# The first sequence's rows are turned in the last group of the experts, and TensorE works the experts' stage in written order

## The chip, the cores and the metric

The kernel runs on one core of one Trainium2 chip. Its time is the device time of that core in microseconds (us) from start to end of one execution; the time before is the median of three runs. Beside them one further execution was profiled, and every line and duration shown comes from that one. TensorE is called PE in the profile, VectorE DVE, ScalarE ACT, GpSimd POOL and SyncE SP; PEld is PE's loading of weights.

## The reference, cut to what matters

Four steps are added to x in turn, 32 sequences of 256 tokens with 128 features: causal attention of 16 heads, a mixture of 16 experts and a shared one, attention by hyperbolic distance, and a feed-forward. The two in the middle are what the change touches (all in fp32):

```python
# experts: 16 of width 64, the best 4 (of the best 2 of 4 groups) weighted, and a shared expert
g = einsum('th,eih->eti', xn, gate_proj);  u = einsum('th,eih->eti', xn, up_proj)
y = einsum('tkh,tk->th', einsum('eti,ehi->eth', silu(g) * u, down_proj)[topk_idx], topk_weight)
x = x + y + (silu(xn @ sg.T) * (xn @ su.T)) @ sd.T

# hyperbolic attention, 16 heads of 8; c = 1
q, k, v = (heads(layernorm(x) @ w.T) for w in (wq, wk, wv))
diff_sq = |q|^2 + |k|^2 - 2 q.k
denom   = maximum((1 - |q|^2) * (1 - |k|^2), 1e-6)
dist    = arccosh(maximum(1 + 2 * diff_sq / denom, 1))
x = x + (softmax(-dist) @ v) @ wo.T
```

Since exp(-arccosh(z)) is z - sqrt(z^2 - 1), a weight of the softmax is such a difference, and its sum comes with the product with the values by a column of ones. Where all |q|^2 and |k|^2 are large enough, the bounds of `denom` and of `z` never act, and 1 / (1 - |q|^2) can be worked into the rows of the queries and keys beforehand. That is the "far path".

## The kernel before, in words

The 8192 tokens are 16 groups (g) of 512; a group is 4 tiles of 128 tokens, or two sequences. x lies in SBUF from the start to the end. The stages follow each other: causal attention (PE in an order written by hand), then experts with the survey, then a branch, then the far path (or another path, which this data does not take).

**Experts (L658).** The first and second layers of two experts at a time make one chunk (c) of 128 rows: 8 chunks and the shared expert, 9 per group. Per chunk there are the products g (L696) and u (L698) into PSUM, Silu on ACT (L700), the multiplication with u (L701) and with the routing weights wb (L703) on DVE, and the product that sums into y (L704). The routing weights come by DMA: each is spread over 64 partitions, 2 MB per group, fetched by SP at chunk 1 of the group before into one of three buffers. When a group's nine sums are done, ACT copies y (L708), PE transposes it and DVE adds it to x (`add_transposed`, L109 and L110). Between them lie the pieces of the routing of the last four groups (`preparation`), one after every odd chunk while there are any.

**Survey (L605).** Of each group, once its x is done: statistics on DVE (L612, L613), x less its mean on POOL (sxn, L614), four transposes on PE (xc, L620), a copy on ACT (L622) and a store of the centred, turned rows to DRAM (L623), the product with the query and key weights in two halves (sqk, L628), its squares on ACT (L633), their sums by head on DVE (L634); then the group's smallest and largest norm (L638, L639) and ra = 1 / (1 - norm) (L641, L642). `survey_result` (L644) makes one flag of all groups' extremes, and the branch at L1451 reads it.

The order of this stage on each engine is not the written one: a planner takes the instructions and sets the order per engine by its own costs. It can put a group's first products between the last steps of the group before.

**Far path (L987).** It is in written order on PE, ACT, DVE and POOL. The rows of queries and keys of one sequence are made in one tile each, qa and ka: a head has 32 places, of which 8 hold the scaled query or key (`scaled`, L1070, with the factors co = ra / deviation), two hold the "last rows" (`last_rows`, L1075 to L1078: a - 1 and a for the query, -0.5 b and 0.5 - 0.5 b for the key; four operations on POOL), and the rest stays zero. `turned` (L1103) transposes them four heads at a time, so that the score product (L1123) has tokens along the free dimension. For one step, a quarter of a sequence's heads, there follow: scores on PE, -4 x scores clipped at zero on ACT (ft, L1177), a product on DVE (fv, L1183), a root on ACT (L1188), the difference on POOL in four operations (L1193), and the product with the values on PE (fav, L1135). The scores of the next step wait for this step's DVE product, since each has its PSUM buffer for itself. The start is outside the loop, in `run` (L1292): the centred rows of group 0 are loaded, sequence 0 is multiplied, scaled and turned, sequence 1 multiplied and scaled, and then the first scores are made.

Of the kernel before, what the change touches and what calls it, by code (L numbers as in the profile page):

```python
# [9 lines left out]
F32 = mybir.dt.float32  # L10
# [6 lines left out]
P = 128  # L17
# [23 lines left out]
class Net:  # L41
# [551 lines left out]
    def survey_tiles(self, keep, dram):  # L593

        self.w_qkv, self.w_o = self.load(keep, "w_qkv", self.nc.sync), self.load(keep, "w_o", self.nc.sync)

        self.xc = [dram.tile([P, GT], F32, name=f"xc{g}") for g in range(NG)]

        self.rv = keep.tile([P, NG, TG], F32, name="rv")
        self.ra = keep.tile([P, NG, TG, 2, H], F32, name="ra")  # L600

        self.ends = keep.tile([P, 2, NG], F32, name="ends")
        self.flag = keep.tile([1, 1], mybir.dt.int32, name="flag")

    def survey(self, pool, psum, g):  # L605

        nc = self.nc
        mv = pool.tile([P, TG, 2], F32, tag="smv", name=f"smv{g}")
        xn = pool.tile([P, TG, D], F32, tag="sxn", bufs=1, name=f"sxn{g}")
        for t in range(TG):  # L610
            st = pool.tile([P, nc.vector.BN_STATS_DIM], F32, tag="sst", bufs=4, name=f"sst{g}_{t}")
            nc.vector.bn_stats(st, self.xg[g][:, t, :])  # L612
            nc.vector.bn_aggr(mv[:, t, :], st)  # L613
            nc.gpsimd.tensor_scalar(xn[:, t, :], self.xg[g][:, t, :], mv[:, t, 0:1], None, ALU.subtract)  # L614
        rv = self.rv[:, g]
        nc.vector.tensor_scalar(rv, mv[:, :, 1], EPS, None, ALU.add)
        nc.vector.reciprocal(rv, rv)
        ps = psum.tile([P, GT], F32, tag="w", name=f"xc_ps{g}")
        for t in range(TG):
            nc.tensor.transpose(ps[:, t * P : (t + 1) * P], xn[:, t, :], self.ident)  # L620
        xc = pool.tile([P, GT], F32, tag="sxc", name=f"sxc{g}")
        nc.scalar.copy(xc, ps)  # L622
        nc.sync.dma_start(out=self.xc[g], in_=xc)  # L623
        n2 = pool.tile([P, TG, 2 * H], F32, tag="sn2", name=f"sn2_{g}")
        for i in range(2):
            qk = psum.tile([P, 2, 2 * D], F32, tag="w", name=f"sqk{g}_{i}")
            for t in range(2):
                nc.tensor.matmul(  # L628
                    qk[:, t], xc[:, (2 * i + t) * P : (2 * i + t + 1) * P], self.w_qkv[:, 0 : 2 * D],
                    start=True, stop=True,  # L630
                )
# [3 lines left out]
                n2[:, 2 * i : 2 * i + 2], sq.rearrange("p t (h d) -> p t h d", d=DH), AX.X, ALU.add  # L635
            )
        nc.vector.tensor_mul(n2, n2, rv.unsqueeze(2).to_broadcast([P, TG, 2 * H]))
        nc.vector.tensor_reduce(self.ends[:, 0, g : g + 1], n2, AX.XY, ALU.min)  # L638
        nc.vector.tensor_reduce(self.ends[:, 1, g : g + 1], n2, AX.XY, ALU.max)  # L639
        ra = self.ra[:, g].rearrange("p t s h -> p t (s h)")  # L640
        nc.vector.tensor_scalar(ra, n2, -1.0, 1.0, ALU.mult, ALU.add)  # L641
        nc.vector.reciprocal(ra, ra)  # L642
# [15 lines left out]
    def experts(self, prep):  # L658
# [3 lines left out]
        with (  # L662
# [18 lines left out]

            pieces = self.preparation(NG // QUAD - 1, prep, psum, "w")
            ready = fetched(0)
            for g in range(NG):
                xT, wb = ready
                y_ps = psum.tile([P, GT], F32, tag="y", name=f"y_ps{g}")
                for c in range(NCH + 1):
                    if c == 1 and g + 1 < NG:
                        ready = fetched(g + 1)
                    shared = c == NCH  # L690
                    m = INTER if shared else P
                    wg = s_g if shared else w_g[:, c * P : (c + 1) * P]
                    wu = s_u if shared else w_u[:, c * P : (c + 1) * P]
                    wd = s_d if shared else w_d[:, c, :]
                    g_ps = psum.tile([P, GT], F32, tag="g", name=f"g_ps{g}_{c}")
                    nc.tensor.matmul(g_ps[:m, :], wg, xT, start=True, stop=True)  # L696
                    u_ps = psum.tile([P, GT], F32, tag="u", name=f"u_ps{g}_{c}")
                    nc.tensor.matmul(u_ps[:m, :], wu, xT, start=True, stop=True)  # L698
                    act = pool.tile([P, GT], F32, tag="act", bufs=3, name=f"act{g}_{c}")
                    nc.scalar.activation(act[:m, :], g_ps[:m, :], AF.Silu)  # L700
                    nc.vector.tensor_mul(act[:m, :], u_ps[:m, :], act[:m, :])  # L701
                    if not shared:
                        nc.vector.tensor_mul(act, act, wb[:, c])  # L703
                    nc.tensor.matmul(y_ps, wd, act[:m, :], start=c == 0, stop=shared)  # L704
                    if c % 2 == 1 and pieces:
                        pieces.pop(0)()
                yT = pool.tile([P, GT], F32, tag="yT", name=f"yT{g}")
                nc.scalar.copy(yT, y_ps)  # L708
                self.add_transposed(pool, psum, "u", g, yT)
                self.survey(pool, psum, g)  # L710
# [276 lines left out]
    def far_attention(self):  # L987
# [20 lines left out]
        with (  # L1008
# [3 lines left out]
        ):  # L1012
            vas = []
# [5 lines left out]

            qa = wp.tile([P, 2, H, ROWS], F32, name="fqa")  # L1020
            ka = wp.tile([P, 2, H, ROWS], F32, name="fka")
            nc.vector.memset(qa, 0.0)
            nc.vector.memset(ka, 0.0)
# [14 lines left out]
            xcs = {}  # L1038

            def centred(g):  # L1040
                xcs[g] = pool.tile([P, GT], F32, tag="xc", name=f"fxc{g}")
                nc.sync.dma_start(out=xcs[g], in_=self.xc[g])
# [13 lines left out]
            def queries_keys(b):  # L1056
                g, ts = chunks(b)
                qk = bank([P, 2, 2, D], f"fqk{b}")
                for t in range(2):
                    i = ts.start + t  # L1060
                    nc.tensor.matmul(
                        qk[:, t], xcs[g][:, i * P : (i + 1) * P], w_qkv[:, 0 : 2 * D], start=True, stop=True
                    )
                return qk.rearrange("p t s (h d) -> p t s h d", h=H)

            def scaled(b, heads, co):
                g, ts = chunks(b)
                for s, x in enumerate((qa, ka)):
                    f = co[:, ts, s].unsqueeze(3).to_broadcast([P, 2, H, DH])
                    nc.vector.tensor_mul(x[:, :, :, 0:DH], heads[:, :, s], f)  # L1070

            def last_rows(b):
                g, ts = chunks(b)
                a, k = (self.ra[:, g, ts, s].unsqueeze(3) for s in range(2))
                nc.gpsimd.tensor_scalar(qa[:, :, :, 8:9], a, 1.0, None, ALU.subtract)  # L1075
                nc.gpsimd.tensor_copy(qa[:, :, :, 9:10], a)
                nc.gpsimd.tensor_scalar(ka[:, :, :, 8:9], k, -0.5, None, ALU.mult)
                nc.gpsimd.tensor_scalar(ka[:, :, :, 9:10], k, -0.5, 0.5, ALU.mult, ALU.add)  # L1078
# [19 lines left out]
            def turned(b, x, hg):  # L1098

                ps = bank([P, 2, N], f"fT_ps{b}_{hg}")  # L1100
                for j in range(2):
                    for t in range(2):
                        nc.tensor.transpose(  # L1103
                            ps[:, j, t * P : (t + 1) * P],
                            x[:, t, (hg + j) * HG : (hg + j + 1) * HG, :].rearrange("p h r -> p (h r)"),
                            self.ident,
                        )
                return ps
# [180 lines left out]
            oTs, sas, sTs, cos = {}, {}, {}, {0: factors(0)}  # L1289
            centred(0)  # L1290

            def run():  # L1292
                scaled(0, queries_keys(0), cos[0])
                last_rows(0)
                rows_of = row_tiles(0)
                for x, to in ((ka, rows_of[1]), (qa, rows_of[0])):
                    for hg in range(0, NHG, 2):
                        (nc.scalar.copy if hg else nc.vector.tensor_copy)(to[hg // 2], turned(0, x, hg))
                last_rows(1)
                scaled(1, queries_keys(1), cos[0])  # L1300
                sc = scores(0, 0, rows_of)

                fours = {}
                for n in range(NHG * (B + 2)):
# [18 lines left out]
                    if s in (1, 2):  # L1323
                        if ahead is not None:
                            nc.vector.tensor_copy(next_rows[s % 2][0], turned(ahead, (qa, ka)[s % 2], 0))
# [7 lines left out]
                    if s in (1, 2):  # L1333
                        if ahead is not None:
                            nc.scalar.copy(next_rows[s % 2][1], turned(ahead, (qa, ka)[s % 2], 2))  # L1335
# [17 lines left out]
                    elif s == 3 and begun is not None:  # L1353
                        scaled(begun, queries_keys(begun), cos[begun // 2])
# [13 lines left out]
                    if s == 2 and begun is not None:  # L1368
                        last_rows(begun)
# [137 lines left out]
```

## Time and profile before

| | us |
|---|---|
| median of three runs (lowest, highest) | 2210.81 (2207.41, 2212.19) |
| the profiled execution, own time | 2204.17 |
| its span in the profile | 2202.4 |
| PE busy in the span | 2063.9 (94%) |
| DVE busy | 1517.5 (69%) |
| ACT busy | 1376.4 (62%) |
| POOL busy | 753.8 (34%) |

Read by the starts of instructions, from the span's beginning: the first product of the experts starts at 1036.20, the flag is made at 1517.83, the first work of the far path starts at 1519.66, its first scores at 1533.61, and it lasts to the end.

In the lines below, L704 is line 704 of the kernel before. A line of the chain of waits has a start, a duration and what ran; a line in order of time has a start, a duration, engine, line, operation, tile written <- tiles read, shapes, the number of alike instructions that were put together, and in brackets how long the engine had been idle and what ended that. A row of a table by stage has the stretch, its length and for each engine the busy time and the number of instructions. Granted clock is the share of full speed that PE was given.

### The profile page before, as it was taken

Reading aid. Unit: us, or ns where it says so; the run is one execution under the profiler, and the core shown is the slowest. Engines: PE = TensorE matmul, PEld = TensorE weight load, DVE = VectorE, ACT = ScalarE, POOL = GpSimd, SP = SyncE. Lnnn points to the kernel's source line nnn. Section 1 sums busy time; section 2 is a strip of 40 time slices with the busy share of each in tenths; the row PEclk is TensorE's granted clock in tenths of the full one; section 3 lists DMA queues with packets and bytes.
Section 4 is the critical chain, followed back from the end, with each engine's and each line's share of the span. In section 5 each row is a group of like instructions: output and inputs, shape, how many; then the busy total and the mean of one; then the engine's idle time right before and its main releaser. Section 6 shows DMA issues by size and latency. Waiting matters only on the chain.

```text
span 2202.4 us, 38323 instructions
## 1 busy us (share of the span) xinstructions
PE 2063.9 (94%) x14083; PEld 1326.1 (60%) x14083; DVE 1517.5 (69%) x4804; ACT 1376.4 (62%) x2429; POOL 753.8 (34%) x841
## 2 busy tenths in 40 slices
PE   5999999999999999997999999996889999999997
PEld 4677777776777777774444433343556565665653
DVE  2666666569655875577558755554678888888885
ACT  1766677666776667663222222222888999999993
POOL 3000000100011000100111100001999999999994
PEclk8999999999999999998999999997899999999999
DMA  5000000000000000001743444400000000000000
GB/s 155 1 1 1 1 1 1 11 11 3 2 6 11 7 2 1 11 11 48 165 96 83 97 96 96 96 10 25 10 6 11 16 11 20 11 15 16 11 11 21
DMA packets 43940, 66.64 MB, mean 30 GB/s; under 512 B 3617, under 2 KB 16689, under 8 KB 43745
## 3 DMA queue, kind: packets, MB, share of 16 engines
q1 hardware_dynamic: 40960, 59.00, 11.2%
q0 software_dynamic: 1200, 3.78, 0.5%
q8 instruction: 114, 1.87, 0.3%
q10 hardware_dynamic: 1584, 1.34, 0.2%
q14 instruction: 82, 0.66, 0.1%
HBM read 50.99 MB, written 13.11 MB: 29 GB/s over the span
## 4 chain that ended last, share of the span: by engine, by line
PE 66%; DVE 14%; ACT 6%; POOL 6%; issue 6%; DMA 1%; POOLq 0%; ACTq 0%; SPq 0%; DVEq 0%
PE t_ps L258 10%; PE s L286 9%; PE y_ps L704 5%; PE fs L1123 5%; PE s L279 4%; PE g_ps L696 4%; DVE fv L1183 4%; PE av L335 4%; PE u_ps L698 3%; PE fav L1135 3%; POOL fv L1193 3%; PE pa_ps L316 3%; ACT ft L1177 2%; PE pb_ps L322 2%; PE pa_ps L315 2%
## 5 line engine op out<-in xcount | busy, mean ns | idle before, releaser
L1193 POOL TENSOR_TENSOR fv<-ft,fv 128x512 f32<-128x512 f32 x512 | 587.8, 1196 | 20.9 <-ACT fv L1188 20.9
L273 DVE CUSTOM_DVE_ANT_0 p<-s,mask 128x128 f32<-128x128 f32 (+1 forms) x1024 | 316.0, 353 | 296.4 <-PE s L279 176.0
L301 ACT ACTIVATE p<-p,lo 128x128 f32<-128x128 f32 (+1 forms) x1024 | 373.6, 444 | 162.8 <-DVE lo L295 162.7
L1183 DVE SCALAR_TENSOR_TENSOR fv<-fs,ft 128x1024 f32<-128x1024 f32 x256 | 300.5, 1216 | 23.3 <-ACT ft L1177 23.3
L1177 ACT ACTIVATE ft<-fs 128x1024 f32<-128x1024 f32 x256 | 247.9, 1020 | 49.1 <-PE fs L1123 40.1
L286 PE MATMUL s<-xT,tT 128*128 128x256 f32 x1024 | 265.6, 382 | 9.0 <-DVE lo L273 9.0
L258 PE MATMUL t_ps<-xT,m_all 128*128 128x512 f32 x512 | 252.9, 614 | 3.2 <-ACT score L525 1.9
L1188 ACT ACTIVATE fv<-fv 128x2048 f32<-128x2048 f32 x128 | 246.6, 1927 | 0.0
L700 ACT ACTIVATE act<-g_ps 128x512 f32<-128x512 f32 x144 | 85.9, 596 | 233.3 <-PE g_ps L696 219.1
L216 POOL TENSOR_TENSOR x<-x,w_bp 128x512 f32<-128x512 f32 x16 | 21.6, 1348 | 611.1 <-DVE xn L213 553.8
L1123 PE MATMUL fs<-fqT,fkT 32*128 32x256 f32 x2048 | 196.3, 408 | 28.2 <-DVE fv L1183 28.1
L286 PEld LDWEIGHTS s<-xT,tT 128*128 128x128 f32 x1024 | 177.4, 193 | 25.0 <-DVE lo L273 11.6
L1123 PEld LDWEIGHTS fs<-fqT,fkT 32*128 32x128 f32 x2048 | 124.2, 185 | 102.5 <-issue 43.6
L504 POOL TENSOR_SCALAR rxn<-x,rmv,rrstd 128x128 f32<-128x128 f32 x64 | 51.2, 811 | 375.7 <-PE rxT_ps L511 223.2
L614 POOL TENSOR_SCALAR sxn<-x,smv 128x128 f32<-128x128 f32 x64 | 44.8, 716 | 385.1 <-DVE smv L613 265.0
L259 ACT ACTIVATE tT<-t_ps,m_bias 128x512 f32<-128x512 f32 x256 | 161.0, 672 | 21.3 <-PE t_ps L258 20.9
L279 PEld LDWEIGHTS s<-xT,tT 128*128 128x128 f32 x1024 | 134.4, 192 | 60.2 <-issue 56.6
L701 DVE TENSOR_TENSOR act<-u_ps,act 128x512 f32<-128x512 f32 x144 | 97.7, 680 | 97.7 <-PE u_ps L698 89.4
L1135 PE MATMUL fav<-fv,fva 128*32 128x257 f32 x2048 | 142.0, 388 | 12.0 <-ACT fqT L1335 4.7
L696 PE MATMUL g_ps<-bxT,w_w_g 128*128 128x512 f32 x256 | 133.9, 609 | 3.1 <-DMA bxT<-xt 3.1
L258 PEld LDWEIGHTS t_ps<-xT,m_all 128*128 128x128 f32 x512 | 87.1, 192 | 81.2 <-issue 50.5
L704 PE MATMUL y_ps<-act,w_w_d 128*128 128x512 f32 x256 | 134.0, 616 | 1.4 <-DVE act L703 0.5
(222 smaller groups left out, 3678.2 us busy)
## 6 DMA issues: line engine op xcount, KB each, us to landing
wb<-rows SPq DMA_DIRECT2D x30, 1024.0 KB, 8.0
xt<-rxT SPq DMA_DIRECT2D x16, 256.0 KB, 2.0
bxT<-xt SPq DMA_DIRECT2D x16, 256.0 KB, 7.6
xc<-sxc SPq DMA_DIRECT2D x16, 256.0 KB, 2.1
fxc<-xc SPq DMA_DIRECT2D x16, 256.0 KB, 2.7
out<-x SPq DMA_DIRECT2D x16, 256.0 KB, 2.3
x<-in_x SPq DMA_DIRECT2D x8, 256.0 KB, 10.7
x<-in_x POOLq DMA_DIRECT2D x8, 256.0 KB, 10.3
```

The costliest lines, as they stand in the source:

```text
L258: nc.tensor.matmul(ps, m_all[:, h], G["xT"], start=True, stop=True)
L273: nc.vector.tensor_tensor_reduce(out=out, in0=x, in1=m, scale=-scale, scalar=3e38, op0=ALU.add, op1=ALU.min, accum_out=accum)
L279: nc.tensor.matmul(s0[:, j], tT[:, j, o : o + P], xT[:, o : o + P], start=True, stop=True)
L286: nc.tensor.matmul(s[:, l], tT[:, j + l, o + P : o + N], xT[:, o : o + N], start=True, stop=True)
L301: nc.scalar.activation(p[:, l], p[:, l], AF.Exp, bias=lo[:, c, l : l + 1], scale=-1.0)
L696: nc.tensor.matmul(g_ps[:m, :], wg, xT, start=True, stop=True)
L704: nc.tensor.matmul(y_ps, wd, act[:m, :], start=c == 0, stop=shared)
L1123: nc.tensor.matmul(sc[j // 2][:, j % 2, kc], kT[rows, kc * P : (kc + 1) * P], qT[rows], start=True, stop=True)
L1177: nc.scalar.activation(t[i], sc[i], AF.Relu, scale=-4.0)
L1183: nc.vector.scalar_tensor_tensor(v[:, 2 * i : 2 * i + 2, :, 0:N], sc[i], 0.5, t[i], ALU.subtract, ALU.mult)
L1188: nc.scalar.activation(v[:, :, :, 0:N], v[:, :, :, 0:N], AF.Sqrt, scale=-4.0)
L1193: nc.gpsimd.tensor_sub(v[:, j, :, 0:N], t[j // 2][:, j % 2], v[:, j, :, 0:N])
```

## The change

In the experts' stage PE no longer follows the planner but the written order; the other engines are still planned. The written order is new. `hidden` issues the products g and u of a chunk with what ACT and DVE do to them, and hands back its sum, which is issued only when two later chunks have been: `waiting` holds them, also across the end of a group. There are four buffers for `act` instead of three. The addition of y and the survey of group g - 1 are cut into five parts that stand at chunks 2, 4, 5, 6 and 7 of group g; the pieces of the preparation stand at chunks 1, 3 and 8. The transposes of y now take a slot of the PSUM tag "w" instead of "u".

The survey's last part also makes the last rows of all tokens of its group (four POOL operations) and stores them in DRAM (`self.last`).

In the last group, chunks 1, 3 and 8 have the parts of `first_rows`: the factors of sequence 0 (a square root on ACT, POOL's multiplication, loads of group 0's centred rows and last rows from DRAM), its product and scaling, and the turning of its keys; the queries are turned after the last sums, between the centred rows and the survey's product of group 15. The turned rows stay in SBUF (`rows0`), also over the branch.

In the far path qa and ka become one tile, `rows`, which POOL clears instead of DVE. `centred` loads a group's last rows with its centred rows, and `last_rows` becomes two copies on POOL. `run` begins with the scores of sequence 0; sequence 1 is scaled behind them.

```diff
     def survey(self, pool, psum, g):
-            nc.gpsimd.tensor_scalar(xn[:, t, :], self.xg[g][:, t, :], mv[:, t, 0:1], None, ALU.subtract)
...
+        def centred():
...
+        def turned():
...
+        def product(i):
...
+        def ends():
...
+            a, b = (self.ra[:, g, :, s] for s in range(2))
+            last = pool.tile([P, TG, 2, H, 2], F32, tag="slast", name=f"slast{g}")
+            nc.gpsimd.tensor_scalar(last[:, :, 0, :, 0], a, 1.0, None, ALU.subtract)
+            nc.gpsimd.tensor_copy(last[:, :, 0, :, 1], a)
+            nc.gpsimd.tensor_scalar(last[:, :, 1, :, 0], b, -0.5, None, ALU.mult)
+            nc.gpsimd.tensor_scalar(last[:, :, 1, :, 1], b, -0.5, 0.5, ALU.mult, ALU.add)
+            nc.sync.dma_start(out=self.last[g], in_=last)
+
+        return [centred, turned, lambda: product(0), lambda: product(1), ends]
+
+    def last_rows(self, b, last, rows):
+        for s in range(2):
+            self.nc.gpsimd.tensor_copy(rows[:, s, :, :, DH : DH + 2], last[:, b % 2 * 2 : b % 2 * 2 + 2, s])
...
+    def first_rows(self, pool, psum):
...
+        def factors():
+            nc.gpsimd.memset(rows, 0.0)
+            nc.sync.dma_start(out=self.xc0, in_=self.xc[0])
+            nc.sync.dma_start(out=last, in_=self.last[0])
+            nc.scalar.activation(rstd, self.rv[:, 0], AF.Sqrt)
+            self.last_rows(0, last, rows)
+            nc.gpsimd.tensor_mul(
+                self.co0.rearrange("p t s h -> p t (s h)"), self.ra[:, 0].rearrange("p t s h -> p t (s h)"),
+                rstd.unsqueeze(2).to_broadcast([P, TG, 2 * H]),
+            )
+
+        def scaled():
+            self.scaled_rows(0, self.xc0, self.co0, bank([P, 2, 2, D], "fqk0"), rows)
+
+        def turned(s):
+            for i in range(2):
+                ps = self.turned_rows(s, 2 * i, bank([P, 2, N], f"fT0_{s}_{i}"), rows)
+                (nc.scalar.copy if i else nc.vector.tensor_copy)(self.rows0[s][i], ps)
+
+        return [factors, scaled, lambda: turned(1), lambda: turned(0)]
...
     def experts(self, prep):
...
+            def hidden(g, c, xT, wb):
...
+                act = pool.tile([P, GT], F32, tag="act", bufs=4, name=f"act{g}_{c}")
...
+                def add():
+                    if c == 0:
+                        sums[g] = psum.tile([P, GT], F32, tag="y", name=f"y_ps{g}")
+                    nc.tensor.matmul(sums[g], wd, act[:m, :], start=c == 0, stop=shared)
+                    if shared:
+                        yT = sums[g, "T"] = pool.tile([P, GT], F32, tag="yT", name=f"yT{g}")
+                        nc.scalar.copy(yT, sums[g])
+
+                return add
+
+            def finish(g):
+                first, *others = self.survey(pool, psum, g)
+
+                def added():
+                    self.add_transposed(pool, psum, "w", g, sums[g, "T"])
+                    first()
+
+                return [added, *others]
...
+            with tc.manual_schedule(engines={mybir.EngineType.PE}):
+                for g in range(NG):
+                    xT, wb = ready
+                    for c in range(NCH + 1):
+                        if c == 1 and g + 1 < NG:
+                            ready = fetched(g + 1)
+                        waiting.append(hidden(g, c, xT, wb))
+                        if len(waiting) > 2:
+                            waiting.pop(0)()
+
+                        if c == 2 and g:
+                            rest = finish(g - 1)
+                        if c in (2, 4, 5, 6, 7) and rest:
+                            rest.pop(0)()
+                        elif g == NG - 1 and c in (1, 3, 8):
+                            early.pop(0)()
+                        elif c in (1, 3, 8) and pieces:
+                            pieces.pop(0)()
+                *others, last = finish(NG - 1)
+                for f in waiting + others[:2] + early + others[2:] + [last]:
+                    f()
             self.survey_result(pool, psum)
...
             def centred(g):
+                if g:
+                    xcs[g] = pool.tile([P, GT], F32, tag="xc", name=f"fxc{g}")
+                    nc.sync.dma_start(out=xcs[g], in_=self.xc[g])
+                lasts[g] = pool.tile([P, TG, 2, H, 2], F32, tag="last", name=f"flast{g}")
+                nc.sync.dma_start(out=lasts[g], in_=self.last[g])
...
-            oTs, sas, sTs, cos = {}, {}, {}, {0: factors(0)}
+            oTs, sas, sTs, cos = {}, {}, {}, {0: self.co0}
             centred(0)
 
             def run():
-                scaled(0, queries_keys(0), cos[0])
-                last_rows(0)
-                rows_of = row_tiles(0)
-                for x, to in ((ka, rows_of[1]), (qa, rows_of[0])):
-                    for hg in range(0, NHG, 2):
-                        (nc.scalar.copy if hg else nc.vector.tensor_copy)(to[hg // 2], turned(0, x, hg))
-                last_rows(1)
-                scaled(1, queries_keys(1), cos[0])
+                rows_of = self.rows0
+                self.last_rows(1, lasts[0], rows)
                 sc = scores(0, 0, rows_of)
+                scaled(1)
...
-                        last_rows(begun)
+                        self.last_rows(begun, lasts[begun // 2], rows)
```

## The prediction

> **What bounds the kernel now.** I read the page's tenths first, then tables by stage, then the chain of waits, then the instructions in order of time. Columns of the first table: stretch, its length, busy us (and instructions) of PE, PE's weight loads, DVE, ACT, POOL, then granted PE clock, DMA share and GB/s.
>
> ```profile
> 1035.00:1510.00 475.00, 453.06 (x1177) 190.65 (x1177) 288.63 (x612) 130.38 (x221) 58.52 (x80) 0.99 0.40 90
> 1510.00:1545.00 35.00, 18.91 (x93) 13.14 (x93) 13.84 (x26) 11.15 (x15) 6.20 (x20) 0.60 0.13 39
> 1545.00:2160.00 615.00, 579.93 (x5482) 360.49 (x5480) 517.71 (x869) 555.61 (x616) 603.57 (x636) 0.99 0.04 13
> ```
>
> The experts (first row) are bound by PE: DVE is busy 61%, ACT 27%, POOL 12%. The crossing from the survey to the far path (second row) is bound by nothing but order: no engine is busy much over half of it and PE has a clock of 0.60. In the far loop (third row) POOL is nearly full.
>
> Busy PE is not PE at its peak, so I counted one steady group. The chain of waits, from one group's end to the next (start, us, what):
>
> ```profile
> 1304.92 2.71 POOL sxn L614 x4
> 1307.63 0.04 issue
> 1307.68 0.33 PE xc_ps L620
> 1308.01 0.86 PE g_ps L696 x2
> ...
> 1328.61 2.11 PE y_ps L704 x4
> ```
>
> A 512-column product is two records, 0.857 us where nothing waits (0.86 in the line of g). The group is 28.8 us long (1299.81 to 1328.61, the starts of two last sums). Its work: 27 products, 27 x 0.857 = 23.1; four transposes of y, 0.44; four of the centred rows, 0.44; eight records of the survey's product, 1.8 (in order of time it starts at 1308.70 and the next product at 1310.51). Sum 25.8. So 3.0 us of each group are waits. The largest is the POOL line: from the transposes of y to the last transposed row PE waits on x, statistics and POOL's subtraction, about 1.7; the pair of last sums takes 2.11 instead of 1.72 (0.4); the rest is in pieces of 0.13 to 0.25, where a sum waits for a DVE multiply that stands behind the survey's reductions.
>
> **The stage now.** First product 1036.20, last sum ends 1503.50: 467.3. Work: 16 x 25.8, less the last group's survey (2.7) that lies behind, 410.1; the preparation's last quad, four pieces of 1.3, 5.2; six passes at half clock at the start, 2.6. Sum 417.9, so 49 us are waits.
>
> **The change part by part.** *PE in written order with lag* (sums two chunks behind, survey of group g spread over chunks 2 to 7 of g+1, transposes of y two chunks before those of the centred rows). It takes the waits away if each input is ready when its place comes. In the new order, with PE back to back from a group's start: last sum of the group before ends at 5.1, transposes of y are at 7.7, of the centred rows at 13.3, survey's products at 16.3 and 19.7. What the centred rows need, by these lines:
>
> ```profile
> 1302.81 0.60 PE L109 MATMUL y_ps<-ident,yT 128*128 128x128 f32 x4
> ...
> 1304.92 2.70 POOL L614 TENSOR_SCALAR sxn<-x,smv 128x128 f32<-128x128 f32 x4 [26.09 <-DVE smv L613]
> ```
>
> From the transposes of y to the last subtraction 4.8 us (1302.81 to the end of the second line); there are 5.6. The slack is 0.8, down to 0.1 where POOL takes longer (the page's mean of 716 ns for one, x4 = 2.9, against 2.7 here, and DVE's queue in between). It is the tightest place; all others have over 0.7 us more than the trace's durations ask for. I allow 0.2 per group, 3.2 in all. The cover is gone elsewhere: in groups 5 to 8 the preparation and best groups of quad 3 fall in the same 67 us in which DVE has about 68 us of work (43 multiplies at 0.605 = 26, four weight parts of 6.4 = 25.7, x, statistics and reductions 17); before, the two groups with most of it took 33.1 and 31.0 instead of 28.8. I allow 5. *New on PE*: the first sequence's product and turned keys, 0.86 each, 1.7. New stage: 417.9 + 3.2 + 5.0 + 1.7 = 427.8, gain 39.5. From both sides: with no bubble and no DVE jam 49; with 0.8 per group and twice the jam, 49 - 1.7 - 12.8 - 10 = 24.
>
> *Added and hidden.* POOL makes four small operations per group for the last rows (1.1 us: the four of the far path, two of them shown below, take 0.32, 0.23, 0.32 and 0.24), and is busy 2.7 of 28.8: cover 20 us. SP issues one more store per group and a load or two; the loads of the multipliers are issued two groups ahead at 92 GB/s, while the first 30 us of the stage moved 186 GB/s; 10% less time per group asks for 102. ACT takes a square root in group 1, in the order as built between the activations of chunks 3 and 4: two table loads.
>
> ```profile
> 1519.70 1.28 ACT L1032 ACT_TABLE_LOAD   x1 [5.40 <-issue]
> ```
>
> By this row two of them cost 2.6. [...]
>
> *Tail of the survey* (last sum to flag, 1503.50 to 1518.12): eight transposes of the queries now stand on PE between the centred rows and the survey's product, at half clock, and the product waits for a slot that DVE's copy frees: +1.1; POOL's last rows and the store stand ahead of the flag's load: +0.1. Loss 1.2.
>
> *Crossing to the far path.* In order of time:
>
> ```profile
> 1519.66 1.84 POOL L1016 MEMSET fva<- 128x1024 f32 x2 [10.98 <-issue]
> ...
> 1525.79 2.04 PE L1061 MATMUL fqk<-w_w_qkv,fxc 128*128 128x256 f32 x4 [8.00 <-DMA fxc<-xc]
> ...
> 1533.61 1.15 PE L1123 MATMUL fs<-fqT,fkT 32*128 32x256 f32 x16
> ...
> 1535.87 2.36 DVE L1183 SCALAR_TENSOR_TENSOR fv<-fs,ft 128x1024 f32<-128x1024 f32 x2 [1.40 <-ACT ft L1177]
> ```
>
> The first sequence's load, product (second line), scaling and turning go; the scores need nothing but the rows kept on chip and start where the stage starts, about 1519.75 instead of 1533.61: 13.9. Two things come back. The trace has the clock at 0.50 until 1532 and 1.00 at 1534 to 1538, so the 16 scores now run cold: about 2.15 instead of 1.15. [...] And the second sequence's product (1.7 cold) and scaling (0.8) now stand on PE behind the scores and on DVE ahead of the first squares: these start 4.75 after the scores, not 2.26. Squares at 1524.5, with the tail's loss 1525.7, against 1535.87: gain 10.2, net of the tail; range 7 to 13. POOL's start (a 1.84 memset more, by the page's row of that shape, minus its four row operations and co) ends about 1526, its first weights are due about 1533: hidden.
>
> *Far loop.* POOL's four operations per sequence become two copies of twice the size:
>
> ```profile
> 1862.73 0.32 POOL L1075 TENSOR_SCALAR fqa<-ra 128x32 f32<-128x32 f32 x1
> 1862.96 0.23 POOL L1076 COPY fqa<-ra 128x32 f32<-128x32 f32 x1
> ...
> 1863.56 9.16 POOL L1193 TENSOR_TENSOR fv<-ft,fv 128x512 f32<-128x512 f32 x8
> 1873.23 9.19 POOL L1193 TENSOR_TENSOR fv<-ft,fv 128x512 f32<-128x512 f32 x8 [0.51 <-ACT fv L1188]
> ```
>
> Now 0.83 per sequence (1862.73 to 1863.56); two copies, by the COPY row 0.21 each, 0.42. That is 12 us less POOL work over 30 sequences. But POOL waits 0.51 per pair of sequences already, for ACT's roots; the loop runs squares, scores, distances at 4.76 a step on DVE, PE and ACT, and never waits for POOL. I take 0; ends: -12 (POOL is the bound after all), +4 (a copy at 0.35 eats POOL's slack).
>
> **Sum.** 39.5 + 10.2 = 49.7. The profiled execution took 2204.2, so 2154.5; the median of the runs shown, 2210.8, lies 6.6 above it, so 2161.
>
> **Rivals.** *Other waits take the place of the removed ones* (DVE's multiplies or the centred rows are late by 1 to 1.5 us per group): for it, DVE has 17 us of work per group in 26 and the tight place above; against it, four activation buffers and a lag of two. Gain 15 to 29 in the stage, time 2172 to 2186. *The far loop gains too*: for it, POOL has 38.6 us of work in 39.1 per pair; against it, the wait of 0.51. 2149 to 2152. *The crossing gains nothing*, since something else starts late there (POOL's memsets, an instruction stream not yet loaded after the branch; POOL, ACT, SP and DVE all start within 0.15 us of 1519.7, which speaks against it): 2171. *Slower*: the transposes of the centred rows stop PE in every group, because DVE's queue puts multiplies between the sums into x and the statistics. Below 0.8 late it costs nothing; to eat 49.7 over 15 groups it must be 3.3 + 0.8 late, the chain 8.9 us instead of 4.8. From there the kernel is slower: at 10 us, 2227. No row here shows such a queue, except in the groups with the preparation.
>
> **How the numbers follow.** Likeliest .64, its own range 2152 to 2170. Other waits .15, far loop too .13, crossing without gain .05, slower .03. Eight in ten from 2146 (the far loop's gain with a good stage) to 2178 (the middle of the other waits). A difference of 0.2%, 4.4 us, is about what this kernel's measurement can tell from none. Faster .96, same .01, slower .03.
>
> **What would show it.** The experts' stage of 428 us and a steady group of 26.0 to 26.3, with no wait for POOL ahead of its transposes; groups 5 to 8 longer by 1 to 2 each; the first scores within 0.3 of the stage's other starts, taking 2.1; squares' step still 4.76 and POOL waiting about 1.3 per pair. The prediction is wrong if PE's idle time in a steady group stays over 1.5, or if the far pair is not 39.1.

## The result and the profile after

The kernel became slower. Median 2235.93 us (2232.00 to 2237.88) against 2211.44 (four runs of each); the ratio is 1.0112, with a 95% interval of 1.0092 to 1.0132. The prediction was 2161, faster. The profiled execution took 2234.25, with a span of 2232.0 instead of 2202.4: 29.6 longer.

Placed by the starts of the same instructions, in both traces ("squares" is DVE's product fv of a step, made by two instructions):

| from, to | before, us | after, us | difference |
|---|---|---|---|
| start to ACT's copy of the last group's sums | 1503.54 | 1470.28 | -33.3 |
| to the first squares of the far loop | 32.3 | 20.6 | -11.7 |
| first to last squares (128 steps) | 621.7 | 696.3 | +74.6 |
| to the end | 44.8 | 44.8 | 0 |

The two parts that the change was aimed at gave 45. The loop that comes behind them, of which only POOL's last rows and the tiles were touched, took 75. Here is the table by stage of the kernel after (stretch, length, busy us and instructions of PE, PEld, DVE, ACT and POOL, granted PE clock, DMA share, GB/s):

```profile
1305.00:1332.00 27.00, 27.00 (x73) 12.21 (x72) 17.16 (x37) 7.74 (x13) 3.79 (x8) 1.00 0.46 102
...
1545.00:2160.00 615.00, 542.74 (x4923) 337.96 (x4922) 512.39 (x798) 496.88 (x552) 524.87 (x516) 0.93 0.05 14
```

In the experts (first row) PE is busy all the time. In the same 615 us of the far loop as before, every engine does less than it did (PE 580, ACT 556, POOL 604 then), and PE's clock has fallen from 0.99 to 0.93: something stops them all. The chain of waits in one pair of sequences says what:

```profile
1800.82 4.22 DVE fo L1309
...
1805.47 0.48 ACT fxn L1316
1805.95 0.92 ACT ft L1268
...
1806.89 1.24 DVE fv L1274
1808.12 0.14 issue
1808.26 3.21 PE fs L1214 x16
```

`fo` is four numbers per partition of the feed-forward's normalisation, made once per pair. It takes 4.2 us. ACT waits for it, the distances (ft) wait for ACT, DVE's squares for those, and PE, idle for 4.4, then makes its 16 scores in 3.21. Before, at this place of a pair, they took 2.26, a wait of 0.43 included. PE's granted clock is down in that stretch:

```profile
1806.50:1812.50 6.00, 4.24 (x21) 2.92 (x22) 3.41 (x5) 5.56 (x7) 2.86 (x3) 0.50 0.00 0
```

Before, it is 1.00 from 1640 to 2190. In order of time, DVE and POOL at that place, after:

```profile
1844.79 0.44 POOL L673 COPY rows<-flast 128x64 f32<-128x64 f32 x2
...
1845.16 4.62 POOL L1284 TENSOR_TENSOR fv<-ft,fv 128x512 f32<-128x512 f32 x4
...
1845.40 0.17 DVE L1308 RECIPROCAL fr<-fr 128x4 f32<-128x4 f32 x1
1845.60 4.20 DVE L1309 SCALAR_TENSOR_TENSOR fo<-fmv,fr 128x4 f32<-128x4 f32 x1
...
1849.84 0.88 ACT L1316 ACTIVATE fxn<-x,fo,fr 128x128 f32<-128x128 f32 x2 [4.93 <-DVE fo L1309]
```

and before:

```profile
1823.59 0.37 POOL L1075 TENSOR_SCALAR fqa<-ra 128x32 f32<-128x32 f32 x1
1823.71 0.17 DVE L1217 RECIPROCAL fr<-fr 128x4 f32<-128x4 f32 x1
1823.82 0.28 POOL L1076 COPY fqa<-ra 128x32 f32<-128x32 f32 x1
1823.91 0.18 DVE L1218 SCALAR_TENSOR_TENSOR fo<-fmv,fr 128x4 f32<-128x4 f32 x1
1823.99 0.36 POOL L1077 TENSOR_SCALAR fka<-ra 128x32 f32<-128x32 f32 x1
```

Before, fo falls among POOL's four small operations for the last rows. After, these are two copies, done 0.4 us before fo comes, and POOL is in the midst of a run of four differences: fo ends when that run ends. The reciprocal (fr) just ahead of it takes 0.17 in the same run. All sixteen of them, least, median and most in ns, before and then after:

```profile
L1218 DVE SCALAR_TENSOR_TENSOR fo<-fmv,fr x16: 161/185/624, 1626.5 to 2184.2; 128x4 f32<-128x4 f32 x16
```

```profile
L1309 DVE SCALAR_TENSOR_TENSOR fo<-fmv,fr x16: 163/4206/4276, 1584.5 to 2213.2; 128x4 f32<-128x4 f32 x16
```

Eleven of them take 4.2; three end with the first difference (0.60, 0.70, 1.24), and the last two find POOL idle (0.16). Each of the eleven lengthens its own step by 4.0 (9.9 instead of 5.9 between squares) and the next one by 1.4 (6.16 instead of 4.76, in which PE has a clock of 0.50 to 0.72): 44.3 and 15.4. Often a third step is longer too (up to 1.5, 6.7 in all). 3.0 more come from the loop's first four steps, which PE makes at half clock (0.50 until 1512.5). With 5 of smaller differences that is the 74.6.

### The profile page after: what moved, and what is told of

Read it like the earlier page. It is cut to its first block, busy times and chain, and to the rows that moved or that the text cites. A ratio compares the mean times of both kernels' runs of the same rounds, so it can differ in the third digit from the quotient of the medians.

```text
span 2232.0 us, 38400 instructions
## 1 busy us (share of the span) xinstructions
PE 2072.9 (93%) x14083; PEld 1349.3 (60%) x14083; DVE 1562.5 (70%) x4802; ACT 1383.1 (62%) x2432; POOL 764.7 (34%) x843
## 4 chain that ended last, share of the span: by engine, by line
PE 35%; DVE 14%; ACT 3%; POOL 3%; issue 2%; DMA 0%; POOLq 0%; ACTq 0%; DVEq 0%; SPq 0%
DVE fv L1274 6%; PE fs L1214 6%; PE g_ps L778 5%; PE y_ps L790 5%; PE u_ps L780 5%; PE fav L1226 3%; POOL fv L1284 2%; DVE fo L1309 2%; ACT ft L1268 2%; PE ff_ps L1338 2%; PE fo_ps L1236 2%; PE sqk L643 1%; PE fT_ps L693 1%; DVE fh L1333 1%; PE fqk L681 1%
## 5 line engine op out<-in xcount | busy, mean ns | idle before, releaser
L1214 PE MATMUL fs<-fqT,fkT 32*128 32x256 f32 x2048 | 208.7, 437 | 70.5 <-DVE fv L1274 69.0
L279 PE MATMUL s<-xT,tT 128*128 128x128 f32 x1024 | 134.9, 275 | 0.0
L316 PE MATMUL pa_ps<-ident,p 128*128 128x128 f32 x512 | 131.1, 280 | 2.8 <-ACT p L301 2.8
```

What stands on the lines that cost most here:

```text
L279: nc.tensor.matmul(s0[:, j], tT[:, j, o : o + P], xT[:, o : o + P], start=True, stop=True)
L1214: nc.tensor.matmul(sc[j // 2][:, j % 2, kc], kT[rows, kc * P : (kc + 1) * P], qT[rows], start=True, stop=True)
```

## The experiments

Theory P: fo cannot run while POOL is in its run of differences, and the shorter last rows moved it there. Theory U: the new start of the far loop, not the last rows, set the engines' phase. Further theories came with the results. Where several runs are given, the ratio is against the kernel before on the same chip.

**The last rows by four operations again.** In the changed kernel, for the far loop alone:

```diff
-                        self.last_rows(begun, lasts[begun // 2], rows)
+                        self.four_last_rows(begun, rows)
```

with the four lines of the kernel before as `four_last_rows`; likewise for sequence 1.

> The changed kernel with the far loop's last rows made by POOL's four operations from ra, as before (0.83 us per sequence instead of 0.41); all else as changed. Theory P (DVE's fo has two SBUF inputs and waits out POOL's run of four differences unless it falls into a pause of POOL; the shorter pause of two copies ended that): fo takes 0.16 to 0.3 again, the pair of sequences takes 39.1, the profiled execution about 2232 - 66 = 2166, at most 2170. Theory U (the new start of the far loop set the engines' phase, the copies have no part): fo stays at 4.2 in most pairs, time within 8 of 2232.

Measured: 2168.1 median, ratio 0.9822 (0.9789 to 0.9855), profiled 2166.67. A pair takes 39.1, and fo:

```profile
L1318 DVE SCALAR_TENSOR_TENSOR fo<-fmv,fr x16: 161/206/603, 1585.9 to 2143.4; 128x4 f32<-128x4 f32 x16
```

0.4 us of additional POOL work per sequence makes the kernel 68 us faster (64 by the two ratios, each against the kernel before beside it). Theory U falls: the new start is still there.

**The two copies alone, in the kernel before.** The survey makes and stores the last rows, `centred` loads them, and

```diff
-                a, k = (self.ra[:, g, ts, s].unsqueeze(3) for s in range(2))
-                nc.gpsimd.tensor_scalar(qa[:, :, :, 8:9], a, 1.0, None, ALU.subtract)
-                nc.gpsimd.tensor_copy(qa[:, :, :, 9:10], a)
-                nc.gpsimd.tensor_scalar(ka[:, :, :, 8:9], k, -0.5, None, ALU.mult)
-                nc.gpsimd.tensor_scalar(ka[:, :, :, 9:10], k, -0.5, 0.5, ALU.mult, ALU.add)
+                for s, x in enumerate((qa, ka)):
+                    nc.gpsimd.tensor_copy(x[:, :, :, DH : DH + 2], lasts[g][:, ts, s])
```

> The kernel before with only the last rows changed: the survey makes and stores them, the far loop loads them and places them with two copies. Theory P: fo takes 4.2 in 10 to 13 of 16 pairs, each costs 4.0 and 1.4 in the next step, so about +65: 2265 to 2280 profiled. Theory U: nothing of the phase changes, 2200 to 2210.

Measured: 2288.65, ratio 1.0353 (1.0311 to 1.0394), profiled 2289.7; most pairs take 45 to 46.

```profile
L1225 DVE SCALAR_TENSOR_TENSOR fo<-fmv,fr x16: 163/4211/4286, 1633.5 to 2267.5; 128x4 f32<-128x4 f32 x16
```

The number of pairs hit is as forecast, eleven, as in the kernel after. The loss is larger than the 65 forecast: from first to last squares it is 78, of which 59.7 are the two steps counted and 9.4 are third steps, and 5.6 more lie ahead of the loop. It is there without the new order of PE and without the first sequence's rows. So the copies, with the store and the loads that feed them, are enough to cause it.

**fo from operations of one input.** In the changed kernel:

```diff
-                nc.vector.scalar_tensor_tensor(o, ff[g]["mv"][:, :, 0], -1.0, r, ALU.mult, ALU.mult)
+                for t in range(TG):
+                    nc.vector.tensor_scalar(
+                        o[:, t : t + 1], ff[g]["mv"][:, t, 0:1], r[:, t : t + 1], -1.0, ALU.mult, ALU.mult
+                    )
```

> The changed kernel with fo made by four small operations of one SBUF tensor input and a scalar each, in place of one with two. [...]

Measured: 2165.83, ratio 0.9805 (0.9770 to 0.9840). A pair takes 39.14, and the operations, four per pair at the same place inside POOL's run, 0.58 together:

```profile
L1310 DVE TENSOR_SCALAR fo<-fmv,fr x64: 202/205/216, 1587.2 to 2144.6; 128x1 f32<-128x1 f32 x64
```

So it is no semaphore and no late instruction that holds fo up, but what kind of operation it is.

**The written order of PE alone, in the kernel before.** The survey in parts, the delayed sums and the PE order, without first rows, stored last rows or any edit of the far path:

```diff
-                    nc.tensor.matmul(y_ps, wd, act[:m, :], start=c == 0, stop=shared)
...
+            with tc.manual_schedule(engines={mybir.EngineType.PE}):
...
+                        waiting.append(hidden(g, c, xT, wb))
+                        if len(waiting) > 2:
+                            waiting.pop(0)()
```

> The kernel before with the experts' stage in the new written order alone: the survey in parts, sums two chunks behind, no rows of the first sequence, no last rows stored, far path as before. If the parts add up: the stage gives 33 (by the changed kernel's trace), the far loop keeps its 39.1 per pair: 2171 profiled, 2166 to 2176. If a faster stage disturbs what follows (theory U in its wide form), the far loop is longer and the time over 2190.

Measured: 2175.53, ratio 0.9857 (0.9824 to 0.9890), profiled 2174.43. Last group's copy at 1470.24 (before 1503.54), first squares 33.0 behind it (before 32.3), pairs of 39.15. The parts add up; the faster stage disturbed nothing behind it.

**Doses.** To measure the stall by itself, one operation more per pair in the kernel before, in the step after fo's, where POOL is in a run; nothing uses its result:

```diff
+                    if now and s == 3 and b % 2 == 0:
+                        nc.vector.scalar_tensor_tensor(few[2], few[0], -1.0, few[1], ALU.mult, ALU.mult)
```

> The kernel before with one operation more per pair of sequences in the far loop, whose result is used by nothing: a product of two tiles of 128 x 4 in SBUF on DVE, in the last step of each even sequence behind the eviction of the mixed values, some 0.3 us after POOL began a run of four differences. Theory P: it waits for the rest of that run, 3 to 4.3 us, in most of the 16 pairs, and the step after is longer by up to 1.4: 2204 + 50 to 95 = 2254 to 2299 profiled. If fo's stall was its own (its operands, its place ahead of ACT), this one takes 0.2: about 2208.

and with one input, `nc.vector.tensor_scalar(few[2], few[0], -1.0, None, ALU.mult)`:

> As the one with two inputs, but the added operation has one input tile (128 x 4 times a constant). [...] If any small DVE operation in SBUF stalls at that place: 2254 to 2299.

Measured, single runs: 2291.76 and 2293.81, against 2206.68. The first is as theory P had it. The second lies in the range for any small operation stalling there: one input of 128 x 4 waits as long as two. The two groups (least, median, most ns):

```profile
L1362 DVE SCALAR_TENSOR_TENSOR few<-few,few x16: 152/4607/9608, 1558.2 to 2224.1; 128x4 f32<-128x4 f32 x16
```

```profile
L1362 DVE TENSOR_SCALAR few<-few x16: 160/4628/9687, 1560.6 to 2226.3; 128x4 f32<-128x4 f32 x16
```

So "two inputs" was too narrow, and I asked whether everything at that place stalls. `nc.vector.reciprocal(few[2], few[0])` there, and the one-input operation on a single column, `few[0][:, 0:1]`:

> As the two doses before, the added operation a reciprocal of 128 x 4 in SBUF. The dose of one input stalled as the one of two did, so two inputs are not what counts. [...] Theory S (anything put at that place stalls): 2254 to 2299.

> As the dose of one input, on one column (128 x 1) of the same tile. [...] If fo from columns escaped only by its other time and place: 2254 to 2299.

Measured, single runs: 2205.51 and 2209.34, against 2207.58.

```profile
L1362 DVE RECIPROCAL few<-few x16: 165/165/169, 1552.0 to 2139.0; 128x4 f32<-128x4 f32 x16
```

```profile
L1362 DVE TENSOR_SCALAR few<-few x16: 140/141/144, 1556.2 to 2143.2; 128x1 f32<-128x1 f32 x16
```

All four stand at the same place of the program and, but for the last of each, start while POOL is in its differences; the kind of operation and its size decide. And the stalls end where POOL lets go: in the kernel after, in the two copies alone and in the two doses that stall, every fo or added operation that took over 0.5 us ended within 0.03 of the end of one of POOL's differences.

That DVE waits for POOL's differences is shown by this (4.2 in the median for fo in the kernel after and with the two copies alone, 4.6 for the two doses that stall); by what means it waits, no trace here shows. Nor is it shown why a scaling of four columns waits (4.63) and one of a single column (0.14) or a reciprocal of four (0.17) does not. And the wait is mostly not for the difference under way alone: one takes 1.19, fo's wait lasted 3.5 of them in most pairs, and a dose's up to 9.7 us.

**The run of differences broken.** Does fo get through where something else than a difference stands between two of them? In the changed kernel, POOL clears 8 columns of an unused tile between the four differences of that step (a clear writes that tile and reads nothing):

```diff
                 for j in range(HG):
+                    if j and broken:
+                        nc.gpsimd.memset(pause, 0.0)
```

> The changed kernel; in the step in which fo is made, POOL clears 8 columns of an unused tile between its four differences (three clears of about 0.1 us, which write and read nothing). [...]

Measured, a single run: 2237.5 (the kernel before beside it 2213.7). Order of time, POOL and then DVE:

```profile
1850.15 1.19 POOL L1288 TENSOR_TENSOR fv<-ft,fv 128x512 f32<-128x512 f32 x1
1851.27 0.12 POOL L1287 MEMSET pause<- 128x8 f32 x1
1851.33 1.19 POOL L1288 TENSOR_TENSOR fv<-ft,fv 128x512 f32<-128x512 f32 x1
...
1853.70 1.19 POOL L1288 TENSOR_TENSOR fv<-ft,fv 128x512 f32<-128x512 f32 x1
1859.51 1.19 POOL L1288 TENSOR_TENSOR fv<-ft,fv 128x512 f32<-128x512 f32 x1 [4.62 <-ACT fv L1279]
```

```profile
1850.59 4.31 DVE L1313 SCALAR_TENSOR_TENSOR fo<-fmv,fr 128x4 f32<-128x4 f32 x1
```

Three clears in between let nothing through; fo ends when POOL has no more work (1854.90), since its next roots wait, by way of ACT, for fo itself. In most pairs fo waits as long as without the clears (4.33 in the median of the sixteen, against 4.21). That it gets through only where POOL has no more work is not the whole rule: in three pairs of the kernel after, fo ended with the first difference (0.60, 0.70 and 1.24), and before, among four small operations without a pause, it took 0.16 to 0.26, against 0.16 where POOL was idle. What decides when fo gets through stays open.

**fo earlier.** In the changed kernel, the reciprocal and fo right behind the root on ACT, ahead of three other evictions:

```diff
                         ff_root(fresh)
+                        ff_factors(fresh)
...
-                            if s == 2:
-                                ff_factors(fresh)
```

> The changed kernel, its one-operation fo kept, but reciprocal and fo issued right behind the root on ACT. fo then starts some 0.6 us before the end of POOL's run, with the copies of the last rows next. Theory P: it waits 0.5 to 0.7 and no more, the pair takes 38.6 to 39.6: 2155 to 2172. If the order on DVE has no part in it: 2225 to 2235.

Measured: 2154.09, ratio 0.9760 (0.9743 to 0.9777). A pair takes 38.7, the time is just below the forecast range, and ACT waits for fo in three pairs only:

```profile
L1309 DVE SCALAR_TENSOR_TENSOR fo<-fmv,fr x16: 163/716/1541, 1580.7 to 2130.9; 128x4 f32<-128x4 f32 x16
```

The same work in another order on one engine is 82 us faster than the changed kernel (78 by the ratios).

The same with fo from four columns:

> fo from one input, and the deviation's reciprocal and fo issued right behind the root on ACT, ahead of the step's other evictions on DVE. Theory Q: what is left of the long step (5.9 instead of 4.8, once per pair) is ACT's wait for fo ahead of the distances; with fo early ACT has 5.4 of work in that step, so 0.4 to 1.0 less per pair, 2155 to 2160. If the long step is ACT's work alone or DVE's place for fo delays others, 2163 to 2172.

Measured: 2158.91, ratio 0.9760 (0.9729 to 0.9791), pairs of 38.57. The step that was 5.9 long is 5.36: theory Q holds for 0.55 per pair.

**PE kept busy over the last group's end.** With fo from four columns, 69 transposes of the identity that nothing uses, in PE's waits:

```diff
+                def busy(n):
+                    ps = psum.tile([P, GT], F32, tag="g", name=f"busy{n}")
+                    for t in range(n):
+                        nc.tensor.transpose(ps[:, t % TG * P : (t % TG + 1) * P], self.ident, self.ident)
...
+                busy(16)
...
+                busy(40)
...
+                busy(13)
```

> fo from one input, and 69 transposes of the identity, used by nothing, in PE's waits between the last group's centred rows and the first scores (16 ahead of the turned queries, 40 behind the survey's last product, 13 behind the flag). Theory C (the slow start of the far loop is PE's clock, fallen in these waits): clock near 1.00 there, 16 first scores in 1.1 to 1.3 instead of 2.1, the second and third step 4.8 instead of 6.3, first eight steps 39 to 40 instead of 41 to 43, tail shorter by 0.5 to 1: 2165 - 3 to -5. Rival: the slow steps come from the loop's filling (loads of the next rows, POOL's start): clock changes and steps stay, 2165 to 2167.

Measured: 2160.81, ratio 0.9775 (0.9748 to 0.9801). By the table by stage the clock stays at 1.00, but not for long:

```profile
1485.00:1490.00 5.00, 4.74 (x49) 4.08 (x47) 2.17 (x10) 0.06 (x1) 1.09 (x4) 1.00 0.07 26
1490.00:1495.00 5.00, 2.37 (x16) 1.61 (x12) 3.02 (x4) 3.82 (x6) 3.88 (x9) 0.96 0.64 141
1495.00:1500.00 5.00, 3.98 (x20) 2.86 (x20) 1.74 (x3) 2.83 (x4) 0.77 (x3) 0.50 0.47 152
```

The first scores take 1.15 instead of 2.09, and from the last sums' copy to the first squares it is 18.7 instead of 21.4. Then PE waits for those squares (busy 2.37 of 5.00), the clock falls to 0.50, and the second and third step take 6.3 each, against 5.9 and 5.2 without the transposes. Theory C is right for the first scores; for the steps after, the clock did not stay up. Of the gain between the two traces (5.8; medians 5.0), 2.6 lies ahead of the first squares and 3.4 behind the last, a stretch that the transposes do not touch and that takes 42.9 to 47.7 in the traces here. So no more than 2.6 can be called theirs, and the intervals overlap.

Both together:

> fo from one input and early, and PE kept busy over the last group's end. If the two gains add: 2159 less 3 to 5, 2153 to 2157. Rival: the busy PE gave only noise (its slow second and third steps stayed), 2157 to 2161.

Measured: 2152.31 (2145.74 to 2156.58), ratio 0.9739 (0.9716 to 0.9762). Against the same without the transposes (2158.91) it is 6.6 less, but the ratios' intervals overlap (0.9760 there), and it is not told apart from the early fo in one operation (2154.09). I would keep that one, which adds no work and leaves both kernels behind.

## Why the prediction was wrong, by its own steps

*The far loop* is the step that failed: "I take 0; ends: -12, +4". It priced POOL's last rows as work on an engine that was not the bound. Their price was right (0.41 for two copies, 0.42 forecast). What they did for another engine was not in it: DVE's fo was due while they ran, and could get through among them (0.16 to 0.26), but mostly not in the differences behind them (4.2). Of the 16 fo before, 12 start 0.19 to 0.51 us after the first of the four operations, which last 0.89 to 0.96 there. Halving them, with POOL some 0.5 earlier against fo, put fo 0.4 us into the run of differences. The prediction's own sign came true: the far pair is not 39.1 but 45.2 in the median. The rival "slower" was put at a place (the centred rows) that gave no trouble. The runs say +68 (taken away) and +81 (alone, by the medians) for the two copies, where the bounds held +4.

*PE in written order* had the right mechanism and was sized 6 too high: 39.5 forecast, 33.3 measured, and 33.3 again with the order alone. The chain of waits after shows a group without any wait, and yet 26.5 long, not 25.8:

```profile
1301.15 0.86 PE sqk L643 x4
1302.02 0.86 PE g_ps L778 x2
...
1304.59 1.00 PE g_ps L778 x2
1305.60 0.86 PE u_ps L780 x2
1306.45 1.06 PE y_ps L790 x2
```

The shared expert's products have 64 rows instead of 128, and where PE goes over to such a product and back, four products take 1.00 to 1.06. I had counted these 0.73 per group as waits that would go (the pair of last sums, "2.11 instead of 1.72"): 11.7 over the stage. The preparation's pieces cost 1.3 in each of six groups, 7.7, not 5.2. Against this the bubbles (3.2) and the jam on DVE (5) did not come: the two groups with DVE busy 26.6 and 26.7 us took 27.9 and 27.7, like their neighbours (27.8). The slack of the centred rows held in all but two groups, which lost 0.7 together. Two readings were off without an effect on the sum: the upper end of 49 leaves out the new work of 1.7, and the longest group before took 32.2 from last sum to last sum, not 33.1.

*The crossing*, 10.2 forecast, net of the tail, gave 11.7. In order of time, after:

```profile
1484.65 0.28 DVE L744 TENSOR_REDUCE flag<-flag_ps 1x1 int32<-1x128 f32 x1 [0.45 <-PE flag_ps L743]
...
1485.93 2.09 PE L1214 MATMUL fs<-fqT,fkT 32*128 32x256 f32 x16 [1.31 <-DVE flag L744]
...
1490.89 2.35 DVE L1274 SCALAR_TENSOR_TENSOR fv<-fs,ft 128x1024 f32<-128x1024 f32 x2
```

The scores start 1.3 after the flag's making, run cold in 2.09 as weighed (2.15), and the squares come 4.96 behind them (4.75). The tail's loss was 0.1, not 1.2. What was missing is that PE stays cold: the clock is at 0.50 until 1512.5, and the first four steps are 3.0 longer than before.

*The rest.* SP's loads and POOL's survey operations cost nothing, as said. ACT's square root is in no term of the sum and cost nothing either: its two table loads took 1.28 each, as the row had it, the next activation started 1.29 after the second one did, and the group in which they fall took 26.52 from one copy of the sums to the next, as long as the steady one. The sum without the failed step would have been 2204.2 - 33.3 - 11.7 + 3.0 = 2162 profiled; with the last rows as before it measured 2166.67.

## What to carry to other kernels

Work that is taken off an engine with slack can still cost (68 us here, by the medians). Here POOL's small operations (0.89 to 0.96 us for the four) were the time in which another engine's operation got through (0.16 to 0.26); in the differences behind them it took 4.2. Before shortening such operations, look at which of the other engine's operations fall into them, at their least and most duration, and at what stands next in both queues. A 0.2 us operation that now and then lasts as long as a neighbour's whole run (4.2 here) is the sign; give it another form (0.58 here, for four operations) or another place in its queue (0.72 here, in the median), and not the neighbour.

## What was not expected of the hardware

- A DVE operation on 128 x 4 waited for the rest of a run of POOL's 512-column differences, 4.2 us in the median and up to 9.7, and in most cases not for the one of 1.19 alone that was under way; with clears of 0.12 between them it still waited 4.33 in the median.
- Scaling four columns stalled (median 4.63), scaling one did not (0.14), nor did a reciprocal of four (0.17), all at one place.
- Behind the stall of 4.2 us on DVE shown above, for which PE waited 4.4, PE's granted clock was 0.50: the next 16 scores took 3.21 instead of 2.26. The step behind such a stall was 1.4 longer (6.16 instead of 4.76).
